# Graph attention kernel: three mask quarters and half of the first graph's heads move from ahead of the steps to between the steps

## The chip, the cores and the metric

The kernel runs on one core of one Trainium2 chip. The metric is the time of one launch in device microseconds (us), the median of several runs. A separate, profiled execution gives the trace; its times are given from the start of its span.

## The reference

Eight graphs of 2048 nodes and 256 channels share one adjacency matrix of 2048 x 2048 integers. For each graph, one attention layer with eight heads of 32 channels, a feed-forward part and three layer norms are computed, all in float32:

```
qkv = einsum('fnc,ck->fnk', x, w_qkv)            # q, k, v: 8 heads of 32
scores = einsum('fnhd,fmhd->fhnm', q, k) / sqrt(32)
scores = where(adj > 0, scores, -1e9)
attn = softmax(scores)
t = einsum('fhnm,fmhd->fnhd', attn, v)
x1 = layernorm(x + t)
x2 = layernorm(x1 + relu(x1 @ w1 + b1) @ w2 + b2)
out = layernorm(x + x2)
```

## The kernel before

**Steps.** The work is cut into 1024 items (f, qc, g, mb): 8 graphs f, 4 quarters qc of 512 query nodes, 2 halves g of the heads (4 heads each) and 16 blocks mb of 128 key nodes. The loop at the end of `fast_path` (L552 on) makes one step per item, in this order. A step t issues the exponentials of item t+1 (L237, ScalarE, 128 x 2048 in one instruction), the scores of item t+2 (`LEAD` is 2), the products with the values of item t (L249, TensorE) and the adding-up of item t (`add_up`). `scores` (L222) is four heads' matmuls on TensorE (L230) and two adds on VectorE (L233), which add the mask and write the sum into a tile `p` of the pool `pp`; the exponentials are made in place in that tile.

**Tiles p.** The pool `pp` has 12 buffers of 128 x 2048 float32. A new tile takes the buffer that has been free longest in program order, and its first writer waits for the last user of the tile before it. The softmax denominators are sums of all exponentials of one (f, qc, g), 16 tiles. `add_up` reduces these 16 to four: blocks 3, 6, 8, 11, 13 and 15 are added into the tile of block 0 on GpSimd (L271), blocks 4, 7, 10 into the tile of block 1 and blocks 5, 9, 12 into that of block 2 by accumulating DMAs that GpSimd issues (L268). Within a chain one accumulation waits for the one ahead of it. So a moved tile's buffer is free when its DMA has landed, and a pooled tile's when GpSimd has added it. `denominator` (L295, matmuls with ones at L310) closes a group a few steps after its last block and frees the other four tiles.

**Masks.** The mask of one quarter qc is the transposed adjacency as fp8 values that are added to the scores: eight pieces of 128 x 2 x 512, each of which serves two blocks mb. `begin` makes all four quarters, in 16 blocks (qc, c) of 512 x 512: a 1 MB load of the adjacency (L511), two conversions to bf16 on VectorE (L528, 128 x 1024 each), 16 transposes on TensorE (L141), and two evictions from PSUM to fp8, one by ScalarE (L147) and one by VectorE (L145). Each piece is written to a DRAM tensor `md` (L148) by the SP queue. The pieces of quarter 0 stay in the pool `mkp` (9 buffers); for every later quarter, and for every later graph, `load_mask` (L150) reads them back, from step 17 of the 32 steps of a quarter on.

**Ahead of the steps.** For the first graph `begin` also loads x (L517), transposes it (`turn_rows`, L95), and makes the queries, keys and values: with block (0, c) those of heads g = 0 (`project`, L200, from `channels` and the value matmuls, all TensorE records at L54), with block (1, c) those of heads g = 1. The scores of items 0 and 1 stand behind block (1, 3); the blocks of quarters 2 and 3 stand behind them and ahead of step 0.

**Side work.** Everything else (projections, transposes, feed-forward, norms of finished quarters, denominators) is written as generators in a list `fill`, sorted by due time. `advance(t)` (L457) resumes them at the head of a step, ahead of that step's scores and values. A generator that needs a PSUM bank yields `BANK`; there is one bank for such work, and a budget (`STEP` 2200 per step, `UNIT` 1024) lets through about one piece per step, which is a group of four 512-column matmuls or as much. When something is needed and not there, `advance(..., finish=True)` runs the list without that limit. `NEXT` (L499) starts the next graph's work at fixed steps. [...]

Of the kernel before, what the change touches and what calls it, by code (L numbers as in the profile page):

```python
# [10 lines left out]
F32 = mybir.dt.float32  # L11
# [8 lines left out]
P = 128  # L20
H = 8
D = 32
CH = 512
# [6 lines left out]
BANK, MORE, WAIT, TURNED, ROOM, INPUTS = -1, -2, -3, -4, -5, -10  # L30
STEP, UNIT, TURN, KEPT = 2200, 1024, 1400, 2200

MASKED = -57344.0
CODE = -5.0


# [25 lines left out]
def fast_path(ctx, tc, cst, x, adj, out, RS):  # L62
# [52 lines left out]
    def take(shape, dt):  # L115
        live.pop(0)
        live.append(ld.tile(shape, dt, name="in"))
        return live[-1]

    def give(t):  # L120
        live[:] = [None if u is t else u for u in live]


    MD = dp.tile([NCK, MB // 2, P, 2 * CH // 4], I32, name="md")
    MK = {}

    def words(mask):
        return mask.rearrange("p b q -> p (b q)").bitcast(I32)

    def mask_piece(t, qc, k):  # L130
        MK[t, qc, k] = mkp.tile([P, 2, CH], F8, name="mask")
        return MK[t, qc, k]

    def mask_blocks(qc, mc, cv, to=None):
        for half in range(2):
            yield BANK
            ps = bank(BF16)
            for r in range(2):
                for j in range(TPC):
                    rr = 2 * half + r  # L140
                    nc.tensor.transpose(ps[:, r, j * P:(j + 1) * P], cv[:, j, rr * P:(rr + 1) * P], identb)  # L141
            k = 2 * mc + half
            m = to[half] if to else mask_piece(0, qc, k)
            if half:
                nc.vector.tensor_tensor(m, ps, cst["ones"][:, 0:1, None].to_broadcast([P, 2, CH]), ALU.min, saturate=False)  # L145
            else:
                nc.scalar.copy(m.bitcast(I8), ps)  # L147
            nc.sync.dma_start(MD[qc, k], words(m))  # L148

    def load_mask(f, qc, k):  # L150
        nc.sync.dma_start(words(mask_piece(f, qc, k)), MD[qc, k])
# [5 lines left out]
    def queries(f, c, xT):  # L157
        for g in range(2):
            yield from channels(QT, qp, "qT", (f, c, g), xT, g * P)

    def turn_rows(xc, xT):
        for a in range(2):
            yield BANK
            ps = bank()
            transposes(ps, [xc[:, j, a * P:(a + 1) * P] for j in range(TPC)])
            nc.scalar.copy(xT[:, a, :], ps)  # L166
# [14 lines left out]
    def channels(store, pool, name, key, xT, k0):  # L181
        yield BANK
        ps = bank()
        for a in range(2):
            if a:
                yield MORE
            columns(ps, wqkv[:, a, k0:k0 + P], xT[:, a, :], start=(a == 0), stop=(a == 1))
        store[key] = pool.tile([P, CH], F32, name=name)
        nc.scalar.copy(store[key], ps)
# [10 lines left out]
    def project(f, c, g, xT=None):  # L200
        if xT is None:
            xT = yield from reload(f, c)
            while len(KT) < (2 * f + g) * NCK + c:
                yield 1
        yield from channels(KT, kp, "kT", (f, c, g), xT, C + g * P)
        yield BANK
        ps = bank()
        for j in range(TPC):
            if j:
                yield MORE  # L210
            for a in range(2):
                columns(ps[:, j * P:(j + 1) * P], xT[:, a, j * P:(j + 1) * P],
                        wqkv[:, a, 2 * C + g * P:2 * C + (g + 1) * P], start=(a == 0), stop=(a == 1))
        v = vp.tile([P, TPC, P], F32, name="v")
        nc.scalar.copy(v, ps.rearrange("p (j c) -> p j c", c=P))
        V[f, c, g] = v
        give(xT)
# [4 lines left out]
    def scores(item):  # L222
        f, qc, g, mb = item
        pt = PT[item] = pp.tile([P, 4, CH], F32, name="p")
        ps2 = [score_pair() for _ in range(2)]

        for half in (1, 0):
            for j in range(2):
                r = D * (2 * half + j)
                nc.tensor.matmul(ps2[half][:, j, :], KT[f, mb // TPC, g][r:r + D, (mb % TPC) * P:(mb % TPC + 1) * P],  # L230
                                 QT[f, qc, g][r:r + D, :], start=True, stop=True)
        for half, ps in enumerate(ps2):
            nc.vector.tensor_tensor(pt[:, 2 * half:2 * half + 2, :], ps,  # L233
                                    MK[f, qc, mb // 2][:, mb % 2, None, :].to_broadcast([P, 2, CH]), ALU.add)

    def exponentials(item):
        nc.scalar.activation(PT[item], PT[item], AF.Exp, scale=1.0 / math.sqrt(D))  # L237
# [249 lines left out]
                resume(e, t)  # L487

    items = [(f, qc, g, mb) for f in range(F) for qc in range(NCK) for g in range(2) for mb in range(MB)]
    LEAD = 2  # L490
    FRAME = 2 * NCK * MB


# [7 lines left out]
            104: [(project, 0, 1)], 108: [(project, 1, 1)], 112: [(project, 2, 1)], 116: [(project, 3, 1)]}  # L501

    def begin():
        todo = deque((qc, c) for qc in range(NCK) for c in range(NCK))
        rows, cols = [], deque()

        def fetch():
            if todo:
                qc, c = todo.popleft()
                t = pp.tile([P, 4, CH], F32, name="p").bitcast(I32)  # L510
                nc.sync.dma_start(t, adj[qc * CH:(qc + 1) * CH, c * CH:(c + 1) * CH].rearrange("(j p) m -> p j m", p=P))  # L511
                cols.append((qc, c, t))

        for c in range(NCK):
            rows.append(pp.tile([P, 4, CH], F32, name="p"))
            xc = rows[c][:, 0:2, :].rearrange("p a (b c) -> p (a b) c", c=C)
            nc.sync.dma_start(xc, x[0, c * CH:(c + 1) * CH, :].rearrange("(j p) c -> p j c", p=P))  # L517
            fetch()
        fetch()
        while cols:  # L520
            qc, c, col = cols.popleft()
            if c % 2 == 0:
                two = pp.tile([P, 4, CH], F32, name="p").rearrange("p a q -> p (a q)").bitcast(BF16)
            cv = two[:, c % 2 * TPC * CH:(c % 2 + 1) * TPC * CH].rearrange("p (j m) -> p j m", m=CH)

            for half, what in enumerate((CODE, MASKED)):
                part = slice(half * 2 * P, (half + 1) * 2 * P)
                nc.vector.tensor_scalar(cv[:, :, part], col[:, :, part], 0.0, what, op0=ALU.is_le, op1=ALU.mult)  # L528
            fetch()
            xT = rows[c][:, 2:4, :]  # L530
            if qc == 0:
                yield from turn_rows(rows[c][:, 0:2, :].rearrange("p a (b c) -> p (a b) c", c=C), xT)
                nc.sync.dma_start(XD[0][c], xT)
                XT[0, c] = xT
                if c == 0:
                    yield from queries(0, 0, xT)
                yield from project(0, c, 0, xT)
            elif qc == 1:
                yield from project(0, c, 1, xT)
            if qc and c % 2 == 0:  # L540
                out4 = take([P, 4, 2, CH], F8)
                give(out4)
            yield from mask_blocks(qc, c, cv, [out4[:, c % 2 * 2 + i] for i in range(2)] if qc else None)
            if (qc, c) == (1, NCK - 1):
                for k in range(LEAD):
                    scores(items[k])
                exponentials(items[0])

    for _ in begin():
        pass  # L550
    state["side"] = 0
    for t, (f, qc, g, mb) in enumerate(items):  # L552
        if g == 1 and mb % 2 and (f + 1 < F or qc + 1 < NCK):
            load_mask(f + (qc + 1) // NCK, (qc + 1) % NCK, mb // 2)
        for what, *which in NEXT.get(t % FRAME, []):
            to = f if what is ask and which[0] else f + 1
            if to < F:
                at = (0, 0, 0) if what is turn else (which[0], 0, 0) if what is ask else (0, which[1], which[0] * TPC)
                start(t, what(to, *which), t + 3 * MB if what is turn else items.index((to, *at)) - LEAD - 1)
        if t == len(items) - MB // 2:  # L560
            state["rows"] = take([P, TPC, C], F32)
            nc.sync.dma_start(state["rows"], x[f, qc * CH:(qc + 1) * CH, :].rearrange("(p j) c -> p j c", p=P))
        if t:
            advance(t)

        if t + 1 < len(items):
            exponentials(items[t + 1])
        if t + LEAD < len(items):
            nf, _, ng, nmb = items[t + LEAD]
            t0 = t  # L570
            while (nf, nmb // TPC, ng) not in V:
                advance(t0, finish=True)
                t0 += 1
            scores(items[t + LEAD])
        values(items[t])
        add_up(items[t])
        if mb == LAST:
            start(t + 2, denominator(f, qc, g, t + SUM), t + SUM + 4)
# [241 lines left out]
```

## Time and profile before

| | |
|---|---|
| median of 3 runs | 3248.77 us (3247.61 to 3251.02) |
| the profiled execution's own time | 3242.05 us |
| its span | 3240.0 us |
| TensorE / VectorE / ScalarE / GpSimd busy | 3101.0 / 2739.5 / 2435.5 / 2593.3 us |
| exponentials of item 0 and item 1 start | 62.38 us, 94.78 us |
| exponentials of item 32, 64, 96, 128, 160 start | 180.4, 276.3, 370.2, 466.1, 560.8 us |
| exponentials of the last item start | 3171.9 us |

The starts of the exponentials are read from the timeline of ScalarE: the records at L237 are counted in order of time, one per item. They are the milestones by which this document compares stages. In the groups of the profile, a row gives line, engine, operation, output and inputs, the count, the busy time and the mean of one in ns, and then the idle time of that engine just ahead of these instructions and what ended it. A float32 matmul has two records, so eight records at L230 or L249 are one step's four heads.

### The profile page before, as it was taken

To read this page: it belongs to the slowest core of one execution; us is meant where nothing else is said; L and a number is where in the kernel's file an instruction comes from. 1 tells how busy PE (TensorE), PEld (TensorE's weight loads), DVE (VectorE), ACT (ScalarE), POOL (GpSimd) and SP (SyncE) were. 2 spreads that over 40 slices of the span, in tenths; PEclk is the share of its full clock that TensorE was granted. 3 is DMA by queue.
4 is the path that set the end of the run, shared out by engine and by line. 5 is a ranking of instruction groups with operands and counts; after the bars stand their busy time and mean duration, and the time that the engine had idled before them with its cause. 6 is when DMAs were issued, how large, how long until landed. Compare 5 with 4: busy or idle time off the path is not lost.

```text
span 3240.0 us, 68306 instructions
## 1 busy us (share of the span) xinstructions
PE 3101.0 (96%) x28948; PEld 976.0 (30%) x28948; DVE 2739.5 (85%) x3203; ACT 2435.5 (75%) x1937; POOL 2593.3 (80%) x1357
## 2 busy tenths in 40 slices
PE   7899999999999999999999999999999999998994
PEld 4222333323332233322333323323233323332221
DVE  4888888888888888888988888888888888888994
ACT  3667778778778777778777778777778777777773
POOL 0568888788878888788887888888888788878894
PEclk8899999999999999999999999999999999999997
DMA  9688779778879788788788879878788878877773
GB/s 322 147 179 190 182 175 202 176 174 200 181 176 205 171 190 193 158 195 200 177 181 175 184 181 220 177 167 197 175 192 194 180 171 201 181 171 160 168 160 78
DMA packets 153384, 591.57 MB, mean 183 GB/s; under 512 B 15056, under 2 KB 67792, under 8 KB 103920
## 3 DMA queue, kind: packets, MB, share of 16 engines
q0 software_dynamic: 64560, 435.85, 67.2%
q1 hardware_dynamic: 87696, 149.98, 13.1%
q8 instruction: 229, 3.75, 0.4%
q10 hardware_dynamic: 816, 1.31, 0.1%
q14 instruction: 83, 0.68, 0.1%
HBM read 146.67 MB, written 37.75 MB: 57 GB/s over the span
## 4 chain that ended last, share of the span: by engine, by line
PE 75%; DVE 8%; POOL 5%; DMA 4%; issue 4%; ACT 2%; DVEq 0%; ACTq 0%; POOLq 0%
PE s L230 28%; PE x L249 24%; PE x L54 13%; DVE p L233 6%; PE x L310 6%; PE x L95 4%; DMA p<-p 3%; POOL p L271 2%; ACT p L237 2%; DMA mask<-md 1%; POOL y L357 1%; DVE st L278 1%; POOL y L355 0%; POOL y L414 0%; POOL y L412 0%
## 5 line engine op out<-in xcount | busy, mean ns | idle before, releaser
L233 DVE TENSOR_TENSOR p<-s,mask 128x1024 f32<-128x1024 f32 x2048 | 2410.5, 1219 | 360.3 <-PE s L230 202.9
L237 ACT ACTIVATE p<-p 128x2048 f32<-128x2048 f32 x1024 | 1956.3, 1910 | 510.2 <-DVE p L233 456.7
L271 POOL TENSOR_TENSOR p<-p 128x2048 f32<-128x2048 f32 x382 | 1829.5, 4791 | 216.0 <-ACT p L237 213.8
L230 PE MATMUL s<-qT,kT 32*128 32x512 f32 x8192 | 1171.2, 641 | 34.1 <-DVE p L233 29.1
L249 PE MATMUL x<-p,v 128*32 128x512 f32 x8192 | 1092.9, 606 | 16.7 <-ACT p L237 16.7
L268 POOL DMA_DIRECT2D p<-p x384 | 360.1, 957 | 305.5 <-ACT p L237 95.5
L230 PEld LDWEIGHTS s<-qT,kT 32*128 32x128 f32 x8192 | 320.5, 183 | 637.8 <-DVE p L233 580.1
L249 PEld LDWEIGHTS x<-p,v 128*32 128x32 f32 x8192 | 161.3, 108 | 796.4 <-issue 302.6
L310 PE MATMUL x<-p,ones 128*32 128x512 f32 x2016 | 261.1, 594 | 15.9 <-POOL p L271 9.7
L289 ACT ACTIVATE y<-y,nb,rs 128x256 f32<-128x256 f32 x372 | 219.2, 590 | 46.1 <-POOL nb L286 46.1
L54 PE MATMUL x<-in,wqkv 128*32 128x512 f32 x1888 | 243.5, 592 | 0.0
L278 DVE BATCH_NORM_STATS2 st<-y 128x6 f32<-128x256 f32 x372 | 155.2, 417 | 6.2 <-DMA y<-in_x_dram 6.2
L54 PE MATMUL x<-w2s,hT 128*32 128x256 f32 x2048 | 122.8, 381 | 3.3 <-DVE y L436 2.3
L54 PE MATMUL x<-turned,w1s 128*32 128x512 f32 x992 | 122.9, 592 | 0.4 <-ACT in L166 0.4
L54 PEld LDWEIGHTS x<-wqkv,in 128*32 128x32 f32 x3584 | 102.2, 110 | 63.5 <-issue 59.0
L54 PE MATMUL x<-wqkv,in 128*32 128x128 f32 x3584 | 117.2, 273 | 0.0
L310 PEld LDWEIGHTS x<-p,ones 128*32 128x32 f32 x2016 | 64.1, 110 | 171.4 <-issue 136.0
L54 PEld LDWEIGHTS x<-in,wqkv 128*32 128x32 f32 x1888 | 61.7, 110 | 140.9 <-issue 113.7
L283 POOL TENSOR_TENSOR rs<-rs,mhalf 128x4 f32<-128x4 f32 x93 | 97.1, 1044 | 7.7
L54 PEld LDWEIGHTS x<-w2s,hT 128*32 128x32 f32 x2048 | 66.1, 110 | 76.5 <-issue 30.3
L414 POOL TENSOR_TENSOR y<-y,be1b2r 128x1024 f32<-128x1024 f32 x32 | 85.4, 2667 | 0.6
L355 POOL TENSOR_TENSOR y<-y,g2r 128x1024 f32<-128x1024 f32 x31 | 82.7, 2668 | 1.2 <-ACT y L289 1.2
(117 smaller groups left out, 1333.1 us busy)
## 6 DMA issues: line engine op xcount, KB each, us to landing
p<-p POOLq DMA_DIRECT2D x384, 1024.0 KB, 10.5
in<-xd SPq DMA_DIRECT2D x87, 512.0 KB, 10.7
mask<-md SPq DMA_DIRECT2D x248, 128.0 KB, 8.0
y<-in_x_dram POOLq DMA_DIRECT2D x62, 512.0 KB, 8.0
p<-in_adj_dram SPq DMA_DIRECT2D x16, 1024.0 KB, 9.7
out_dram<-y SPq DMA_DIRECT2D x31, 512.0 KB, 6.4
in<-in_x_dram SPq DMA_DIRECT2D x29, 512.0 KB, 15.9
xd<-in SPq DMA_DIRECT2D x28, 512.0 KB, 10.9
```

The costliest lines, as they stand in the source:

```text
L54: nc.tensor.matmul(out[r:r + D], lhsT[:, r:r + D], rhs, start=start, stop=stop)
L95: nc.tensor.transpose(ps[:, j * P:(j + 1) * P], s, ident)
L230: nc.tensor.matmul(ps2[half][:, j, :], KT[f, mb // TPC, g][r:r + D, (mb % TPC) * P:(mb % TPC + 1) * P], QT[f, qc, g][r:r + D, :], start=Tr ...
L233: nc.vector.tensor_tensor(pt[:, 2 * half:2 * half + 2, :], ps, MK[f, qc, mb // 2][:, mb % 2, None, :].to_broadcast([P, 2, CH]), ALU.add)
L237: nc.scalar.activation(PT[item], PT[item], AF.Exp, scale=1.0 / math.sqrt(D))
L249: nc.tensor.matmul(O[grp][r:r + D, :], V[f, mb // TPC, g][:, mb % TPC, r:r + D], PT[item][:, h, :], start=(mb == 0), stop=(mb == LAST))
L268: nc.gpsimd.dma_start(PT[f, qc, g, chain[0]], PT.pop(item), accum_op=ALU.add)
L271: nc.gpsimd.tensor_tensor(first, first, PT.pop(item), ALU.add)
L278: nc.vector.bn_stats(st, t[:, j, :])
L283: nc.gpsimd.tensor_tensor(rs, rs, cst["mhalf"], ALU.pow)
L289: nc.scalar.activation(t[:, j, :], t[:, j, :], AF.Identity, bias=nb[:, j:j + 1], scale=rs[:, j:j + 1])
L310: nc.tensor.matmul(ps[r:r + D, :], cst["ones"], term[:, h, :], start=(n == 0), stop=(n == len(terms) - 1))
```

## The change

`begin` now makes only quarter 0 of the masks and only heads g = 0 of the first graph, and issues the first scores right after. Both evictions of a transposed block are ScalarE's. The four projections of heads g = 1 (with the queries of g = 1 for quarter 0) become a generator `other_half`, one for each c, due at steps 13, 17, 21 and 25. The 12 remaining blocks become generators `mask_quarter(qc + 1, c)`, started at blocks mb 0, 4, 8 and 12 of the g = 0 groups of the first three quarters of graph 0. Each takes one tile `p`, loads its 1 MB into it as two 512 KB DMAs, converts in place five steps later, and transposes, evicts and writes out from the same tile, in two pieces of side work. So a tile `p` is held from the load to the second write to `md`. The four tiles that hold the transposed rows of x are held until their `other_half` has run. `load_mask` is issued six steps later than before (`LATE`), in all graphs, and in graph 0 only after its piece was made. The mask value of VectorE's eviction, `MASKED`, goes.

```diff
+    def mask_quarter(qc, c):
+        t = pp.tile([P, 4, CH], F32, name="p").rearrange("p a q -> p (a q)")
+        half = TPC * CH // 2
+        parts = [t[:, h * half:(h + 1) * half] for h in range(2)]
+        cvs = []
+        for h, part in enumerate(parts):
+            col = part.bitcast(I32).rearrange("p (j m) -> p j m", j=TPC)
+            nc.sync.dma_start(col, adj[qc * CH:(qc + 1) * CH, (2 * c + h) * 2 * P:(2 * c + h + 1) * 2 * P].rearrange("(j p) m -> p j m", p=P))
+        yield 5
+        for part in parts:
...
+            convert(cv, part.bitcast(I32).rearrange("p (a b m) -> p a b m", a=2, b=2))
+            yield 1
+        for h, part in enumerate(parts):
             yield BANK
             ps = bank(BF16)
...
+            turn_mask(ps, cvs[h])
+            m = part[:, half // 4:half // 2].bitcast(F8).rearrange("p (b q) -> p b q", b=2)
+            nc.scalar.copy(m.bitcast(I8), ps)
+            nc.sync.dma_start(MD[qc, 2 * c + h], words(m))
+            MADE.add((qc, 2 * c + h))
...
-    LEAD = 2
+    LEAD, LATE = 2, 6
...
     def begin():
...
+        for c in range(NCK):
...
+            yield from turn_rows(rows[c][:, 0:2, :].rearrange("p a (b c) -> p (a b) c", c=C), xT)
+            nc.sync.dma_start(XD[0][c], xT)
+            XT[0, c] = xT
+            if c == 0:
+                yield from channels(QT, qp, "qT", (0, 0, 0), xT, 0)
+            yield from project(0, c, 0, xT)
+            for half in range(2):
+                ps = bank(BF16)
+                turn_mask(ps, [cv[:, j, half * 2 * P:(half + 1) * 2 * P] for j in range(TPC)])
+                m = mask_piece(0, 0, 2 * c + half)
+                nc.scalar.copy(m.bitcast(I8), ps)
+                nc.sync.dma_start(MD[0, 2 * c + half], words(m))
+                MADE.add((0, 2 * c + half))
+        for k in range(LEAD):
+            scores(items[k])
+        exponentials(items[0])
+        for c in range(NCK):
+            start(0, other_half(c, rows[c][:, 2:4, :]), MB + TPC * c - LEAD - 1)
...
     for t, (f, qc, g, mb) in enumerate(items):
-        if g == 1 and mb % 2 and (f + 1 < F or qc + 1 < NCK):
-            load_mask(f + (qc + 1) // NCK, (qc + 1) % NCK, mb // 2)
+        uf, uqc, ug, umb = items[max(t - LATE, 0)]
+        if ug == 1 and umb % 2 and (uf + 1 < F or uqc + 1 < NCK):
+            while ((uqc + 1) % NCK, umb // 2) not in MADE:
+                advance(t, finish=True)
+            load_mask(uf + (uqc + 1) // NCK, (uqc + 1) % NCK, umb // 2)
+        if f == 0 and mb % TPC == 0 and qc + 1 < NCK:
+            c = g * TPC + mb // TPC
+            if c < NCK:
+                start(t, mask_quarter(qc + 1, c), t + MB + 2)
```

More of the change, by code (lines that the diff above doesn't have):

```diff
@@ L31 @@
 STEP, UNIT, TURN, KEPT = 2200, 1024, 1400, 2200
-MASKED = -57344.0
 CODE = -5.0
@@ L124, in fast_path @@
     MD = dp.tile([NCK, MB // 2, P, 2 * CH // 4], I32, name="md")
-    MK = {}
+    MK, MADE = {}, set()
     def words(mask):
@@ L132, in mask_piece, with turn_mask, convert @@
         return MK[t, qc, k]
-    def mask_blocks(qc, mc, cv, to=None):
-        for half in range(2):
+    def turn_mask(ps, cv):
+        state["credit"] -= 2 * TURN
+        for r in range(2):
+            for j in range(TPC):
+                nc.tensor.transpose(ps[:, r, j * P:(j + 1) * P], cv[j][:, r * P:(r + 1) * P], identb)
+    def convert(cv, col):
+        nc.vector.tensor_scalar(cv, col, 0.0, CODE, op0=ALU.is_le, op1=ALU.mult)
+    def mask_quarter(qc, c):
[8 more added lines that the diff above has]
+        for part in parts:
+            cv = part.bitcast(BF16).rearrange("p (a b m) -> p a b m", a=2, b=4)[:, :, 0:2, :]
+            cvs.append([cv[:, j // 2, j % 2] for j in range(TPC)])
+            convert(cv, part.bitcast(I32).rearrange("p (a b m) -> p a b m", a=2, b=2))
+            yield 1
+        for h, part in enumerate(parts):
             yield BANK
             ps = bank(BF16)
[L138 to L148, printed above, removed]
+            turn_mask(ps, cvs[h])
[3 more added lines that the diff above has]
+            MADE.add((qc, 2 * c + h))
     def load_mask(f, qc, k):
@@ L503, in begin @@
     def begin():
[L504 to L512, printed above, removed]
+        rows, cols = [], []
         for c in range(NCK):
@@ L517, in begin @@
             nc.sync.dma_start(xc, x[0, c * CH:(c + 1) * CH, :].rearrange("(j p) c -> p j c", p=P))
[L518 to L521, printed above, removed]
+            cols.append(pp.tile([P, 4, CH], F32, name="p").bitcast(I32))
+            nc.sync.dma_start(cols[c], adj[0:CH, c * CH:(c + 1) * CH].rearrange("(j p) m -> p j m", p=P))
+        for c in range(NCK):
             if c % 2 == 0:
@@ L524, in begin, with other_half @@
             cv = two[:, c % 2 * TPC * CH:(c % 2 + 1) * TPC * CH].rearrange("p (j m) -> p j m", m=CH)
-            for half, what in enumerate((CODE, MASKED)):
+            for half in range(2):
                 part = slice(half * 2 * P, (half + 1) * 2 * P)
-                nc.vector.tensor_scalar(cv[:, :, part], col[:, :, part], 0.0, what, op0=ALU.is_le, op1=ALU.mult)
-            fetch()
+                convert(cv[:, :, part], cols[c][:, :, part])
             xT = rows[c][:, 2:4, :]
[L531 to L547, printed above, removed]
+            yield from turn_rows(rows[c][:, 0:2, :].rearrange("p a (b c) -> p (a b) c", c=C), xT)
[4 more added lines that the diff above has]
+            yield from project(0, c, 0, xT)
+            for half in range(2):
+                ps = bank(BF16)
[9 more added lines that the diff above has]
+            start(0, other_half(c, rows[c][:, 2:4, :]), MB + TPC * c - LEAD - 1)
+    def other_half(c, xT):
+        if c == 0:
+            yield from channels(QT, qp, "qT", (0, 0, 1), xT, P)
+        yield from project(0, c, 1, xT)
     for _ in begin():
```

## The prediction, as put on record

> **What bounds the kernel now.** I read the page first: its busy times say TensorE.
>
> ```profile
> PE 3101.0 (96%) x28948; PEld 976.0 (30%) x28948; DVE 2739.5 (85%) x3203; ACT 2435.5 (75%) x1937; POOL 2593.3 (80%) x1357
> PEclk8899999999999999999999999999999999999997
> ```
>
> An average over stages, so next the stretches before and after the steps begin (columns: TensorE busy, weight loads, VectorE, ScalarE, GpSimd, granted clock, DMA share, GB/s).
>
> ```profile
> 60.00:80.00 20.00, 9.25 (x72) 6.80 (x72) 13.75 (x16) 5.96 (x5) 0.00 (x0) 0.54 0.79 272
> 80.00:100.00 20.00, 11.54 (x84) 7.52 (x88) 12.15 (x15) 5.86 (x5) 0.00 (x0) 0.52 0.30 93
> 160.00:180.00 20.00, 17.65 (x136) 4.45 (x130) 18.50 (x16) 16.14 (x10) 14.71 (x8) 1.00 1.04 229
> 180.00:200.00 20.00, 15.40 (x112) 3.59 (x112) 12.12 (x11) 10.39 (x7) 13.70 (x4) 0.91 0.83 199
> ```
>
> From 60 to 95 us nothing is near its limit: the last two mask quarters pass through VectorE, TensorE and an eviction one block after another, one in 3.8 us (conversions at 88.20 and 92.06). That is the time the change aims at. Around 180 us there is another hole. The timeline shows its kind:
>
> ```profile
> 190.76 4.52 POOL L271 TENSOR_TENSOR p<-p 128x2048 f32<-128x2048 f32 x1 [2.30 <-ACT p L237]
> ...
> 193.98 0.16 PEld L310 LDWEIGHTS x<-p,ones 128*32 128x32 f32 x8 [5.09 <-DMA p<-p]
> 193.98 1.20 PE L310 MATMUL x<-p,ones 128*32 128x512 f32 x8 [4.18 <-DMA p<-p]
> 195.11 0.52 PEld L230 LDWEIGHTS s<-qT,kT 32*128 32x128 f32 x8 [0.97 <-issue]
> 195.11 2.09 PE L230 MATMUL s<-qT,kT 32*128 32x512 f32 x8
> ```
>
> A late accumulating DMA holds in-order TensorE, and its next instructions take twice their time (2.09 us, not 1.07). In the steps the chain of waits gives 1.07 us for a step's scores, 1.00 for its values and 0.86 for a full side piece: 2.93 us. Without a side piece a step takes 2.55 us, set by VectorE's adds (starts at 127.81, 130.35, 132.91).
>
> How late a tile's buffer comes free is the third thing to read: the first additions of the run on GpSimd, and the row of all tiles p between 96 and 466 us.
>
> ```profile
> 105.17 4.56 POOL L271 TENSOR_TENSOR p<-p 128x2048 f32<-128x2048 f32 x1 [85.46 <-ACT p L237]
> 109.67 1.84 POOL L268 DMA_DIRECT2D p<-p  x2
> DMA to landing us min/median/max: 6.8/10.8/15.6
> ```
>
> Alone an accumulation lands in 7 us; the pair issued from 109.67 had both landed at 123.1, 13.4 us later; the median is 10.8.
>
> **What the Trainium skill says.** "DMA: Bandwidth & Descriptors", SWDGE vs HWDGE: accumulating during a DMA is GpSimd's alone, so L268 can't leave the queue that also adds (L271); and the section "Issuing engines are not separate DMA queues": all queues share the 16 DMA engines. The trace agrees: at a DMA share of 1.04 (160 to 180 us) accumulations took 11 to 16 us. "TensorE: Matmul & The Clock Gate", Part 1: an idle window of about 3.4 us halves the clock; here 0.54 and 0.52 above, and 2.09 us after a hole of 5. "Perfetto Trace Analysis", Optimization Strategy: bubbles that repeat can mean that there is no buffer for the next tile. Before, adds hardly wait for buffers (0.9 us for DMAs between 96 and 466 us).
>
> **The change, part by part** (minus is gain; by the profiled execution, 3242.05 us, span plus 2.05).
>
> *Earlier start.* Before, block (0, 3) left TensorE at 38.96 us. Both evictions are now ScalarE's, 1.01 us each in one queue ahead of the next rows' copies, which have no slack: 3 x 1.07 = 3.2 us later, 42.2. Scores 1.1 and adds 2.5: item 0's exponentials at 45.8, item 1's at 48.4, not 94.78: **-46.4**. The loads of these blocks stand as before on SP, so they don't move.
>
> *TensorE work brought between the steps.* Four projections of 3.46 us (keys 2 x 0.86, values 2 x 0.87), a query piece 1.72, 24 half blocks of 0.54 (16 transposes took 1.07 at 32.08): 13.8 + 1.7 + 12.9 = **+28.4**. By the order of instructions all of it stands ahead of item 160; from there both programs issue the same. The steps there are TensorE's, so it adds fully, except for 18 of the first 32 steps: these had no side piece before and went at VectorE's pace, and all have one now: 18 x (2.55 - 2.07) = **-8.6**. The hole at 194 us should go, as slower steps leave the DMAs time: **-6**. A step with one of the 24 conversions (0.65 us) needs 2.48 + 0.65 = 3.1 of VectorE against 2.93: 24 x 0.2, half of it hidden: **+2**. The 24 casts (1.01) I cost at nothing, since ScalarE idles 25%; without that cover they'd cost 24. Sum without buffers: **-31**.
>
> *Buffers p.* Counting tiles from allocation to last use in program order, before at most 6 of 12 are held in the first 16 steps (heads of the chains, tiles in work), so a buffer is reused 9 items after its tile was given back. After, row tiles and blocks bring this to 10 or 11 through step 21: item 6 takes item 3's buffer, 7 takes 4's, 8 takes 5's, 10 takes 7's, 12 takes 9's, 16 takes 12's. The wait stands on VectorE's add; behind it are the next adds and conversions, on TensorE the next scores (for PSUM), and the exponentials that feed the next accumulation. A moved tile needs exponentials 1.9, queue and landing 7 to 13, but has two steps, 5.9 us. Item by item, from the start of item 0's exponentials: those of item 3 end at 9.7; GpSimd adds to 14.4 (4.7); accumulation 4 lands at 21.4 (+7.0), 5 at 27.8 (14.4 + 13.4). Item 7's adds start at 21.4 (17.0 unhindered), item 8's at 27.8, item 9 runs to 33.1. Accumulation 7 lands 5.5 after 27.8 and 2.7 later for a 1 MB block load: item 10 at 36. Addition 8 ends at 36.9, accumulation 9, with 10 behind it, lands at 45.5: item 12 there, not at 40.5. Accumulation 12 lands near 58.7: item 16. Items 15 and 20 take buffers of blocks, free when the write to `md` lands (3 to 8 us): +3 for item 20; items 24 and 26 +1 each. TensorE restarts slowly after four of these holes, about +0.8 each. So item 32's exponentials start at 45.8 + 117 = 163; unhindered 48.4 + 31 x 2.93 + 2.6 (three steps with a double piece) = 142: **+21**. In quarters 1 and 2 blocks again take tiles and 4 MB of loads (10.8 us of all DMA engines on top of about 40 in 47): reuse distance 3 to 6, accumulations about 3 us later; by the same working waits of 2.3, 1.2, 2 and 4 us in items 43 to 47, and the like in items 70 to 80: **+9 each**. Sum **+39**.
>
> *Mask reads.* Six steps later, 17.6 us; they are then 7 steps, 20.5 us, ahead of use and land in 8.1 (24.8 at most): **0**; without that cover some us a quarter.
>
> Total -31 + 39 = **+8**: 3250 for a profiled run. The median of the runs is 6.7 above the profiled execution, so 3248.8 + 8 = **3257**.
>
> The disputed size is the waits: at landings of 7 us and quick writes the first group costs 14 and the others 4 each (22); at 15.6 us each, 40 and 15 each (70). I take 39: solo landings in the stalled group, the shared pair where two overlap.
>
> **Rivals.** (1) *Faster: the early start outlives the waits.* If buffer waits stay under 31 us in all, time falls; at 15 us, as when TensorE catches up at VectorE's 2.5 us a step after each hole, 3233. For it: an idle front of 35 us is real, and before no buffer wait is seen. Against: the reuse distance falls from 9 to 3. (2) *Slower by much: DMAs bind.* With 53 us of transfers in a 47 us group, chained accumulations slip as at 178 us (15.6), waits reach 63: 3281. Against: the block loads come early, when no accumulation runs. (3) *Even*: waits near 31, 3249. (4) *Not done*: steps don't start sooner because SP's block loads hold `begin`. Against: TensorE waited for such a load only once before, at 19 us.
>
> **How the numbers follow.** Forecast 0.50 (3250 to 3268), rival 1 0.24, rival 2 0.14, rival 3 0.10, rival 4 0.02. About 0.2%, 6.5 us, is what can be told from no change. Faster by over that: most of rival 1, 0.21. Within: rival 3 and the edges of the forecast and rival 1, 0.25. Slower: 0.54. The forecast's own range and the rivals' centres give 3231 to 3284.
>
> **What would show it.** Item 1's exponentials at 48; item 32 near 163 (142 if rival 1); VectorE idle at the adds ended by DMA or GpSimd at tiles p, some 20 us before item 32 (0.9 before); item 160 near 569, not 561, and from there equal lengths. Item 160 under 550 makes the prediction wrong.

## The result, and the profile after

The changed kernel takes 3266.5 us (median of 6 runs, 3262.86 to 3274.01), the kernel before 3248.31 in the same job (6 runs, 3247.05 to 3251.02). The ratio is 1.0061, 95% interval 1.0051 to 1.0070: 18 us slower, more than twice the 8 that were forecast. That is on the forecast's side and near the upper end of its range (3250 to 3268).

In the page of the changed kernel, the lines that answer to the two shown of before:

```profile
PE 3108.9 (95%) x28948; PEld 976.5 (30%) x28948; DVE 2741.3 (84%) x3187; ACT 2448.8 (75%) x1953; POOL 2594.8 (79%) x1357
PEclk9999999999999999999999999999999999999997
```

The totals hardly differ. The clock row no longer begins with two eights: the slow front is gone. What came for it is below the row's resolution (one slice is 82 us), so here are stretches of 20 us of the changed kernel, the first two of them at the times shown of before:

```profile
60.00:80.00 20.00, 14.53 (x148) 4.61 (x144) 10.62 (x10) 8.83 (x7) 8.96 (x6) 0.83 0.77 156
80.00:100.00 20.00, 15.52 (x172) 5.91 (x168) 12.83 (x13) 11.78 (x8) 11.47 (x6) 0.91 0.90 200
...
200.00:220.00 20.00, 14.52 (x104) 3.98 (x102) 13.29 (x10) 11.69 (x9) 11.20 (x5) 0.83 1.03 247
320.00:340.00 20.00, 11.35 (x86) 3.78 (x86) 18.23 (x14) 10.21 (x10) 14.08 (x5) 0.74 0.75 184
```

(The columns are those of the stretches of before: busy TensorE, weight loads, VectorE, ScalarE, GpSimd, granted clock, DMA share, GB/s.) At 60 to 100 us the steps now run, though with holes. At 200 to 220 us TensorE is idle a quarter of the time while the DMA engines are full (1.03). At 320 to 340 us TensorE is idle for 8.7 us and VectorE is busy for 18.2 of the 20: another kind of hole. That suggests two causes, and the milestones (starts of the exponentials, by item) say how much each stage lost, in us. The forecast's column is taken from its working: 142 - 48.4 - 85.6 = +8 and +21 for waits in the first stage, -6 and +9 in the second, +9 in the third. What is left of the TensorE work (28.4 - 8.6 + 2 - 8) is put at the stage up to item 160; the working says only that it stands ahead of that item.

| stage | before | after | difference | forecast |
|---|---|---|---|---|
| start to item 1 | 94.8 | 48.6 | -46.2 | -46.4 |
| item 1 to 32 | 85.6 | 113.9 | +28.3 | +29 |
| 32 to 64 | 95.9 | 107.0 | +11.1 | +3 |
| 64 to 96 | 93.9 | 113.4 | +19.5 | +9 |
| 96 to 160 | 190.6 | 206.8 | +16.2 | +13.8 |
| 160 to the last | 2611.1 | 2606.8 | -4.3 | 0 |
| sum | 3171.9 | 3196.5 | +24.6 | +8.4 |

The sum of two single traces is 24.6, the medians differ by 18.2. The profiled run of before was 6.7 us under its median and that of after (3266.33) at its own, so about 6 us of this table can't be given to a stage. Some of it lies in the first row: in the traces of E2, E3, E4 and E11 below, which share before's front, item 1 starts at 96.4 to 97.9 us, not at 94.8.

First kind of hole: VectorE's waits (total in us, times, longest), of before between 96 and 466 us and then of the change between 45 and 383 us.

```profile
DVE p L233 <- DMA p<-p: 0.9, 1, 0.9
...
DVE p L248 <- DMA p<-p: 22.1, 9, 6.4
DVE p L248 <- PE s L245: 21.5, 31, 1.9
DVE p L248 <- DMA md<-p: 5.1, 3, 2.5
...
DVE p L248 <- POOL p L286: 1.3, 2, 0.8
```

L248 (L233 in before) is the mask add that first writes a new tile `p`. It waits for an accumulation, a write to `md` or a pooled add to give the buffer back: 28.5 us, where before had 0.9. 19.5 of it lies ahead of item 32. Its first four, from VectorE's timeline:

```profile
69.36 2.36 DVE L248 TENSOR_TENSOR p<-s,mask 128x1024 f32<-128x1024 f32 x2 [6.38 <-DMA p<-p]
74.23 2.36 DVE L248 TENSOR_TENSOR p<-s,mask 128x1024 f32<-128x1024 f32 x2 [1.92 <-DMA p<-p]
82.41 2.35 DVE L248 TENSOR_TENSOR p<-s,mask 128x1024 f32<-128x1024 f32 x2 [2.62 <-DMA p<-p]
90.99 4.84 DVE L248 TENSOR_TENSOR p<-s,mask 128x1024 f32<-128x1024 f32 x4 [2.77 <-DMA p<-p]
```

These are items 7, 8, 10 and 12. The prediction had them at 21.4, 27.8, 36 and 45.5 us after 45.8, which is 67.2, 73.6, 81.8 and 91.3. The later and smaller waits of this stage stand at items 15, 20, 24 and 26 (1.3, 1.3, 1.6 and 0.9 us), all of which the prediction names; at item 16, which it names too, none is seen.

Second kind: the conversions. Their row in before (up to 200 us: busy time, mean ns), their summary in the change (L140: shortest, median and longest in ns, first and last start), and the worst of them in the timeline of VectorE, GpSimd and TensorE:

```profile
L528 DVE TENSOR_SCALAR p<-p 128x1024 bf16<-128x1024 int32 x32 | 20.8, 692 | 12.8 <-DMA p<-in_adj_dram 12.8
...
L140 DVE TENSOR_SCALAR p<-p x32: 675/684/9233, 19.3 to 345.2; 128x1024 bf16<-128x1024 int32 x32
```

```profile
318.70 3.22 POOL L370 TENSOR_TENSOR y<-y,g2r 128x1024 f32<-128x1024 f32 x1
319.99 9.23 DVE L140 TENSOR_SCALAR p<-p 128x1024 bf16<-128x1024 int32 x1
321.03 5.34 POOL L286 TENSOR_TENSOR p<-p 128x2048 f32<-128x2048 f32 x1
325.50 3.16 POOL L372 TENSOR_TENSOR y<-y,be2r 128x1024 f32<-128x1024 f32 x1
...
330.41 2.09 PE L245 MATMUL s<-qT,kT 32*128 32x512 f32 x8 [8.65 <-DVE p L248]
```

The median conversion takes 0.684 us. This one starts while GpSimd is in an instruction and ends 0.56 us after the third of three in a row (325.50 + 3.16 = 328.66; 319.99 + 9.23 = 329.22). Behind it in VectorE's order stand the mask adds, so TensorE waits 8.65 us, and its next scores take 2.09 us instead of about 1.1. Of the 24 conversions between the steps, five are stretched like this (4.38, 3.53, 4.07, 3.31, 9.23 us) and one slightly (1.10). These six, and none of the other 18, started while GpSimd was in an add or multiplication of two tiles. Above 0.68 us each, the 24 take 3.7 us too much ahead of item 32, 6.7 in quarter 1 and 11.2 in quarter 2, 21.6 in all. In before no conversion stood beside GpSimd's adds of tiles `p`: all were done before the steps. The Trainium skill ("SBUF — State Buffer", section "Who interferes with whom") describes it: VectorE and GpSimd share a pair of ports that is taken for a whole instruction, `tensor_scalar` is among those that can use it, and "the other **fully blocks** (not throttle)". The trace agrees, with 4.38 us where GpSimd's one add ended 3.83 us after the conversion's start and 9.23 us where three followed each other. The prediction took the duration from rows without such a neighbour.

### The profile page after: what moved, and what is told of

Same layout as the page of the kernel before. It is cut to its first block, busy times and chain, and to the rows that moved or that the text cites. A ratio compares the mean times of both kernels' runs of the same rounds, so it can differ in the third digit from the quotient of the medians.

```text
span 3264.5 us, 68367 instructions
## 1 busy us (share of the span) xinstructions
PE 3108.9 (95%) x28948; PEld 976.5 (30%) x28948; DVE 2741.3 (84%) x3187; ACT 2448.8 (75%) x1953; POOL 2594.8 (79%) x1357
## 4 chain that ended last, share of the span: by engine, by line
PE 72%; DVE 4%; POOL 3%; issue 3%; ACT 1%; DMA 1%; DVEq 0%; ACTq 0%; POOLq 0%
PE s L245 26%; PE x L264 23%; PE x L53 14%; PE x L325 5%; PE x L94 4%; DVE p L248 3%; POOL p L286 1%; ACT p L252 1%; POOL y L372 1%; DMA p<-p 0%; POOL y L370 0%; DVE st L293 0%; DVE y L360 0%; POOL y L374 0%; DMA y<-in_x_dram 0%
## 5 line engine op out<-in xcount | busy, mean ns | idle before, releaser
L248 DVE TENSOR_TENSOR p<-s,mask 128x1024 f32<-128x1024 f32 x2048 | 2409.3, 1218 | 410.6 <-PE s L245 215.6
L325 PE MATMUL x<-p,ones 128*32 128x512 f32 x2016 | 260.5, 595 | 12.7 <-POOL p L286 10.5
L53 PE MATMUL x<-w2s,hT 128*32 128x256 f32 x1920 | 115.4, 381 | 0.0
L372 POOL TENSOR_TENSOR y<-y,be2r 128x1024 f32<-128x1024 f32 x31 | 84.2, 2715 | 0.0
```

Source lines behind the costliest of these rows:

```text
L53: nc.tensor.matmul(out[r:r + D], lhsT[:, r:r + D], rhs, start=start, stop=stop)
L325: nc.tensor.matmul(ps[r:r + D, :], cst["ones"], term[:, h, :], start=(n == 0), stop=(n == len(terms) - 1))
L372: nc.gpsimd.tensor_tensor(z, z, rows(cst["be2r"]), ALU.add)
```

## Experiments

Ratios are to before in the same job, with 95% intervals; differences in us are of the medians. The expectation of E5 says how it changes the computation; E7 and E8 take over the same form.

**E1, the conversions without the shared port.**

```diff
-            convert(cv, part.bitcast(I32).rearrange("p (a b m) -> p a b m", a=2, b=2))
+            nc.vector.tensor_scalar(cv, part.bitcast(I32).rearrange("p (a b m) -> p a b m", a=2, b=2), 0.0, None,
+                op0=ALU.is_le, op1=ALU.add, accum_out=small.tile([P, 1], F32, name="acc"))
...
-            nc.scalar.copy(m.bitcast(I8), ps)
+            nc.scalar.mul(m.bitcast(I8), ps, CODE)
```

> The changed kernel, but each conversion of a mask block between the steps also sums its output (so it compares only; ScalarE's eviction multiplies by the code). Theory A (the conversion, in the form it has, can't run beside a large GpSimd instruction, and VectorE stands until that ends; together with the waits for tiles p this is the loss): the 24 conversions take 1.1 to 1.3 us each and none is stretched, where the changed kernel has five of 3.3 to 9.2 us; item 160's exponentials start 10 to 20 us sooner than its 589.7; time 3248 to 3257, against 3266.5. Theory B (the waits for tiles p alone are the loss; a stretched conversion only stands where the next add would have waited for a buffer anyway): item 160 within 4 us of 589.7, time 3263 to 3270.

Measured: 3267.02 us, ratio 1.0056 (1.0044 to 1.0069), as slow as the change, with item 160 at 591.9 us: the figures of theory B. The group of its conversions (busy time, mean ns), and VectorE's waits between 45 and 385 us:

```profile
L154 DVE TENSOR_SCALAR_CACHE_REDUCE p<-p 128x1024 bf16<-128x1024 int32 x24 | 29.0, 1208 | 0.0
```

```profile
DVE p L248 <- DMA p<-p: 27.5, 10, 6.3
...
DVE p L248 <- DMA md<-p: 9.4, 4, 3.7
```

None is stretched (1.185 to 1.221 us), though seven of them started during an instruction of GpSimd. That is what the same section says of the form that writes its accumulator. VectorE spends 29 us on them and not 38, but waits 37 us for DMAs and not 27. The stretch is real and not the whole cause: without it no time came back.

**E2, the conversions alone**, on the kernel before, with an unused result. By the order of VectorE's instructions each stands one step ahead of where the change has it (steps 5, 6, 8, 9 and so on, not 6, 7, 9, 10).

```diff
+        if t in (5, 6, 8, 9, 12, 13, 16, 17, 36, 37, 40, 41, 44, 45, 48, 49, 68, 69, 72, 73, 76, 77, 80, 81):
+            nc.vector.tensor_scalar(spare, wqkv[:, :, 0:CH].bitcast(I32), 0.0, CODE, op0=ALU.is_le, op1=ALU.mult)
```

> The kernel before, with 24 conversions of 128 x 1024 added on VectorE (from the weights into a spare tile), at the 24 steps of graph 0 at which the changed kernel has its own; no tile p is taken. Theory A: some are stretched to 3 us and more while GpSimd adds, 10 us or more above 24 x 0.68 in sum, and the time rises by 5 to 15 us, to 3254 to 3263. Theory B: each takes 0.7 us, half hidden: 3248 to 3253.

Measured: 3295.13 us, ratio 1.0134 (1.0119 to 1.0149): +47, three times the most that was expected. One of them in its timeline, with the add that it met:

```profile
116.81 4.54 POOL L272 TENSOR_TENSOR p<-p 128x2048 f32<-128x2048 f32 x1 [1.18 <-ACT p L238]
117.50 4.40 DVE L567 TENSOR_SCALAR spare<-wqkv 128x1024 int8<-128x1024 int32 x1
```

It starts 0.69 us into the add and ends 0.55 after it. The 24 take 46 us together, 30 of it stretch; eleven were hit here, six in the change. Stage by stage the time of the conversions is nearly the time lost: 17, 14 and 15 us of conversions, and 18, 12 and 15 us more from item 1 to 32, to 64 and to 96. So not only the stretch stood in the steps' path, but the plain 0.68 us of each as well.

**E3, the buffers alone**, on the kernel before: 16 extra tiles `p`, held over the steps for which the change holds its rows and blocks (given back one step sooner, by the order of TensorE's instructions), each touched by a tiny DMA and a tiny write.

```diff
+        for a, b in HOLD:
+            if t == a:
+                held[b] = pp.tile([P, 4, CH], F32, name="p")
+                nc.sync.dma_start(held[b][:, 0, 0:4], x[0, 0:P, 0:4])
+            if t == b:
+                nc.vector.memset(held.pop(b)[:, 0, 0:1], 0.0)
```

> The kernel before, with 16 further tiles p allocated and given back at the steps of graph 0 at which the changed kernel allocates and gives back its blocks and its four row tiles; each is only touched by a DMA of 16 bytes per partition and, at its end, by one short VectorE write. Theory A: waits of VectorE for DMAs at tiles p rise from 0.9 us to 15 to 25 us; the kernel is slower by 15 to 25 us: 3263 to 3273. Theory B, in which buffers are all of the loss: slower by 35 to 45 us, 3283 to 3293. If buffers cost nothing: 3248.

Measured: 3275.84 us, ratio 1.0079 (1.0066 to 1.0092): +27, between the two theories' ranges and nearer to A's. VectorE's waits between 96 and 402 us:

```profile
DVE p L233 <- DMA p<-p: 29.2, 10, 4.6
```

Held buffers alone make the waits that the prediction described, without any block load: 12.9 us of them (with one for GpSimd) ahead of item 32, 9.4 and 8.5 in the next two quarters. The stages lost 17.0, 3.3 and 9.7 us from item 1 to 32, to 64 and to 96. The working's terms for buffers and for the hole at 194 us, which is gone in E3 too, give 21, 9 - 6 = 3 and 9.

**E11, both on the kernel before** (the edits of E2 and E3 together).

> The kernel before, early start and all else as it was, with both single costs that were measured apart: the 24 extra conversions on VectorE (their result unused, alone +46 us) and the 16 extra buffers held (alone +26 us). If they stand in different steps they add: 3315 to 3325 us. If a wait for a buffer and a conversion cover each other: 3293 to 3305 us.

Measured: 3290.87 us, ratio 1.0137 (1.0122 to 1.0152): +43, far below the 74 of a sum (47 and 27, where the expectation has 46 and 26) and no more than the conversions alone. VectorE's waits between 97 and 417 us:

```profile
DVE p L234 <- DMA p<-p: 13.5, 5, 4.5
```

The waits fell from 29.2 to 13.5 us and the stretch from 30 to 22. My reading is that accumulations catch up while VectorE stands in a stretched conversion, and that GpSimd's add ends while it waits for a buffer; no run separates this. Shown is that the two don't add, and that both shrank when they stood together.

**E5, the conversions on ScalarE.**

```diff
-            convert(cv, part.bitcast(I32).rearrange("p (a b m) -> p a b m", a=2, b=2))
+            nc.scalar.activation(cv, part.bitcast(I32).rearrange("p (a b m) -> p a b m", a=2, b=2), AF.Identity,
+                bias=cst["code"][:, 0:1], scale=-CODE)
```

> The changed kernel with the 24 conversions between the steps on ScalarE (-5 + 5 x adjacency, which takes the adjacency as 0 or 1). They took 38 us of VectorE in the changed kernel, 16 of work and 22 of standing beside GpSimd. Theory A (conversions stand in the steps' path for nearly their whole time, as they did when added alone): 20 to 35 us less, 3232 to 3247, item 160 at 560 or sooner. Theory B (the waits for tiles p cover them: without conversions VectorE waits for the buffers instead): 0 to 10 us less, 3256 to 3267, VectorE's waits for DMAs at tiles p longer by about as much.

Measured: 3270.5 us, ratio 1.0074 (1.0061 to 1.0087). VectorE has nothing of the conversions left, and waits between 45 and 385 us:

```profile
DVE p L248 <- DMA p<-p: 37.6, 10, 6.4
...
DVE p L248 <- DMA md<-p: 14.6, 4, 5.0
```

That is 52 us of waits for buffers in place of 27: what E11 showed from the other side, and more than theory B had it, for no time came back. Not all of it need be VectorE's absence: ScalarE is busy 254 us between items 1 and 96 where it was busy 230, and the exponentials, which feed the accumulations, start later behind their adds (28 us in sum, 20 in the change). How much of the new waits comes from that is open.

**E6, the heads ahead again** (the masks between the steps alone) and **E10, only the heads between the steps** (all masks ahead, as before).

```diff
             yield from project(0, c, 0, xT)
+            yield from other_half(c, xT)
...
-        for c in range(NCK):
-            start(0, other_half(c, rows[c][:, 2:4, :]), MB + TPC * c - LEAD - 1)
...
```

This is the edit of E6; E10 makes the heads by the same `other_half`, on the kernel before.

> The changed kernel with the second half of the heads made ahead of the steps again (and a missing query tile forced like a missing value tile). The steps start 15.5 us later; the four row tiles are free by then, so 8 tiles p at most are held in the first 16 steps, not 11. Theory A (of the 21 us of waits before item 32 most come from the row tiles): waits in the first group fall to about 7 us, side work of 15.5 us leaves the steps, item 32 within 3 us of the changed kernel's 162.5, and 8 to 15 us less in all for what is then not owed later: 3252 to 3258. Theory B (blocks and their conversions alone make the loss): as the changed kernel, 3263 to 3270.

> The kernel before with the other part of the change alone: all masks are made ahead as before, and only the second half of the first graph's heads is made between steps. If the two parts simply add, this is worth what taking it out of the changed kernel cost (3278.3 against 3266.5, so 12 us): 3235 to 3239 us. If the heads cost between the steps what they cost ahead of them (item 1 about 10 us earlier, item 32 as before), 3245 to 3251 us: the 12 us of the other run then came from the masks between meeting the heads, not from the heads.

E6: 3278.32 us, ratio 1.0100 (1.0085 to 1.0114), slower than the change. E10: 3253.72, ratio 1.0020 (1.0013 to 1.0028). Both expectations missed in both runs. The heads between the steps cost 6 us alone and save 12 in company, so the parts don't add either.

E10 prices the heads' terms one by one. Item 1 comes at 93.6 us, 1.2 earlier than in before's trace and 2.8 to 4.3 earlier than in the four others with its front: as long as the masks of quarters 2 and 3 stand ahead, the heads there cost little. Items 1 to 32 take 8.1 us more (forecast: 13.8 + 1.7 - 8.6 = 6.9). Items 32 to 64 take 5.4 less, which looks like the hole (forecast -6), but only in part is: TensorE's wait for the late DMA fell from 4.2 to 0.7 us, and it ran 698 instructions there where before ran 753. In all it ran 151 fewer between items 32 and 128, and 156 more in items 128 to 160 (1104 for 948), which took 10.0 us more. The side work that the heads displaced comes back there, and the working has no term for it. From item 1 to 160 the heads cost 9.2 us, where 6.9 - 6 = 0.9 was forecast.

E6 gains 9.4 us on the change up to item 32 counted from item 1, but starts 10.6 later, and loses 10.2 and 12.1 in quarters 1 and 2. Its longest single wait, at item 46 in VectorE's timeline, and the landing of its four writes to `md` that were issued between 195 and 230 us:

```profile
223.92 2.35 DVE L248 TENSOR_TENSOR p<-s,mask 128x1024 f32<-128x1024 f32 x2 [17.68 <-DMA md<-p]
```

```profile
DMA to landing us min/median/max: 9.2/15.1/21.1
```

A block's buffer is given back only when its last write has landed. The write that this add waited for was issued at 202.7, right behind two 512 KB block loads that landed 15.5 and 21.2 us after issue, and a reload. In the change the longest such wait is 2.5 us. Why heads between the steps spare it, beyond other moments of loads and writes, is not settled.

**E9, the writes to `md` from ScalarE's queue**, to take them out of the order in which SyncE issues its DMAs.

```diff
-            nc.sync.dma_start(MD[qc, 2 * c + h], words(m))
+            nc.scalar.dma_start(MD[qc, 2 * c + h], words(m))
```

> The changed kernel, with the finished mask pieces' write to DRAM (md from p) issued by ScalarE, right behind the cast that makes them, and not by SyncE, where in the trace of after it stands behind block loads that wait for a buffer. Theory A (SyncE's order keeps the blocks' buffers, and VectorE waits for them): VectorE's waits for DMA md from p (10.6 us in all in after) go to under 3 us, those for DMA p from p shrink, quarters 1 and 2 (items 32 to 96, 220 us in after) get 6 to 12 us shorter: 3254 to 3261 us. Theory B (the DMA engines themselves are full there, and who issues doesn't matter): waits only change names, 3263 to 3270 us.

Measured: 3270.46 us, ratio 1.0068 (1.0055 to 1.0080). (VectorE waits 5.1 us for `md` in the change, not the 10.6 of the expectation.) That wait is 7.5 us here, the one for accumulations 21.1, items 32 to 96 take 220.9 us and took 220.4. SyncE's order isn't the cause: without it the waits are as long, and the writes land in 8.5 us (median between 160 and 385 us), in the change in 8.3. That leaves the full DMA engines, which is argued here and not shown.

**E7 and E8, blocks half as often.** Blocks start every eight steps over both halves of the heads, with conversions on ScalarE; E8 has the heads ahead as in E6.

```diff
-        if f == 0 and mb % TPC == 0 and qc + 1 < NCK:
...
+        if f == 0 and mb % (2 * TPC) == 0 and qc + 1 < NCK:
+            start(t, mask_quarter(qc + 1, g * 2 + mb // (2 * TPC)), t + MB // 2 + 2)
```

> As the run with conversions on ScalarE, and the blocks of a quarter started every 8 steps over both halves of the heads, not every 4 in the first half, due 10 steps later. Held tiles p in the groups of quarters 1 and 2 fall from 8 to 6 or 7 (7 to 10 in the first groups). If tiles are what is left: 5 to 12 us less than the run with ScalarE alone. If not: within 4 us of it.

> All three: conversions on ScalarE, blocks every 8 steps, the second half of the heads ahead of the steps. If conversions and tiles are the whole loss, what is left is the earlier start less the work brought between the steps: 20 to 30 us faster than the kernel before, 3219 to 3229. If something else is lost too (DMAs of the blocks beside the accumulations), 3235 to 3250.

E7: 3274.32 us, ratio 1.0089 (1.0072 to 1.0107), within 4 us of E5 as the second of its expectations had it. VectorE waits 21.9 us for accumulations and 16.7 for `md` (one of 13.3). E8: 3256.6, ratio 1.0028 (1.0019 to 1.0037), the best of this family, still behind before and slower than either expectation. Waits for accumulations are down to 9.6 us there and those for `md` to 1.0. In their place TensorE waits for a reload of the next graph's rows that landed 28.8 us after issue, right behind a block load:

```profile
210.80 1.93 PE L53 MATMUL x<-in,wqkv 128*32 128x512 f32 x8 [15.20 <-DMA in<-xd]
```

**E4 and E12, the late mask reads**: `LATE` = 6 alone on the kernel before, and taken out of the change.

```diff
-    LEAD, LATE = 2, 6
+    LEAD, LATE = 2, 0
```

> The kernel before, with the reads of the mask pieces issued six steps later, in all graphs. Both theories: no change, 3245 to 3252, since the smallest distance between landing and first use in the kernel before is 20 us and six steps are 17.6 us. If late reads cost anything, 1 us in each of 31 quarters gives 3280.

> The changed kernel with one of its three parts undone: a mask piece's read into SBUF is issued at its own step again, as before the change, and not six steps later. If the late reads are worth in the changed kernel what they were worth alone on the kernel before (7 us gained), it gets that much slower: 3271 to 3277 us. If my prediction's zero holds here, or the gain belongs to the first graph's steps that the stalls have taken over: 3263 to 3269 us. If the early reads collide with block loads and accumulations in quarters 1 and 2, items 32 to 96 take over 224 us where they took 220.

E4: 3241.91 us (10 runs, 3237.12 to 3247.49), ratio 0.9977 (0.9968 to 0.9987): faster than both kernels, and the best version found, where no change was expected. Its profiled run took 3245.96 us, at the slow end of its runs, and the table's stages from item 1 on are within about 1 us of before's. So it doesn't show where the 7 us come from; that stays open. E12: 3286.85, ratio 1.0127 (1.0105 to 1.0149), 20 us slower than the change and slower than any of its expectations. Here the trace tells where. Lines of its timeline, at items 26 and 46:

```profile
143.80 2.35 DVE L248 TENSOR_TENSOR p<-s,mask 128x1024 f32<-128x1024 f32 x2 [2.13 <-PE s L245]
...
151.14 1.14 PE L245 MATMUL s<-qT,kT 32*128 32x512 f32 x8
...
152.35 1.23 DVE L248 TENSOR_TENSOR p<-s,mask 128x1024 f32<-128x1024 f32 x1 [6.19 <-PE s L245]
...
227.09 2.36 DVE L248 TENSOR_TENSOR p<-s,mask 128x1024 f32<-128x1024 f32 x2 [11.49 <-DMA md<-p]
```

By the code, an early read that finds its piece not made runs the whole side list at once (the loop on `MADE`). The trace agrees: pieces of keys and of values and two half blocks stand between two steps on TensorE (143.6 to 151.1 us). Counted against the change, E12 falls behind from 1.7 to 8.9 us at item 26, to 11.2 at item 30, and from 10.2 to 18.2 at item 46, of which 4 come back.

## Why the prediction was right, and where its sizes were not

The forecast had the direction and the main mechanism, tiles `p` that are held longer and buffers that come free late. Its sum of +8 came out of sizes that were wrong both ways.

*The start, right.* Item 1 at 48.6 us; forecast 48.4.

*Buffers ahead of item 32, right in kind, place and size.* Item 32 at 162.5 us; forecast 163. Each of the first four waits came within 2.2 us of its place. The waits there are 19.5 us against 21, with 3.7 of stretch beside them that the working did not have. E3 confirms held tiles as a cause by themselves.

*"A step with one of the 24 conversions (0.65 us) needs 2.48 + 0.65 = 3.1 of VectorE against 2.93: 24 x 0.2, half of it hidden: +2": this is the step that failed.* The duration came from rows where GpSimd was idle, and half was taken as hidden. Beside GpSimd's instructions the same instruction took up to 9.23 us: 21.6 us of stretch in the trace of the change, 30 in E2, where hardly anything was hidden: 46 us of conversions, 47 lost.

*"+9 each" in quarters 1 and 2, not as forecast.* The waits for buffers there were 7.9 and 1.2 us, and with the stretch (6.7 and 11.2) 14.6 and 12.4: in quarter 2 the stretch stands where the waits were forecast. Of the 18.6 us by which the two quarters missed (8.1 and 10.5), this gives 9.0 (27.0 against 18). The other 9.6 are not told apart. The same stages of before (three lines) and of the change (three lines), items 32 to 64, 64 to 96 and 128 to 160, columns as above:

```profile
180.40:276.30 95.90, 90.12 (x753) 25.57 (x752) 79.00 (x80) 70.51 (x51) 68.63 (x30) 0.98 0.80 175
276.30:370.20 93.90, 93.68 (x884) 29.35 (x880) 84.06 (x98) 75.06 (x60) 82.91 (x45) 1.00 0.86 187
466.10:560.80 94.70, 94.70 (x948) 30.52 (x944) 84.09 (x98) 74.38 (x59) 83.37 (x44) 1.00 0.85 181
...
162.50:269.50 107.00, 95.02 (x736) 28.53 (x732) 89.86 (x88) 77.49 (x58) 64.11 (x29) 0.94 0.77 188
269.50:383.00 113.50, 98.53 (x804) 30.02 (x800) 99.97 (x106) 80.23 (x66) 84.37 (x44) 0.92 0.83 195
477.60:589.70 112.10, 108.78 (x1260) 39.28 (x1260) 84.53 (x98) 78.79 (x67) 82.71 (x43) 1.00 0.79 174
```

In both quarters TensorE was busy some 4.9 us longer with fewer instructions, at a lower granted clock (0.94 and 0.92, before 0.98 and 1.00). That is about the size of what is left, but no run tests it.

*TensorE's work, right in place, its credits too large.* It stands ahead of item 160 as forecast: items 96 to 160 took 16.2 us more for 13.8, all of it in items 128 to 160 (1260 instructions for 948). But the working took off 8.6 us for steps without a side piece and 6 for the hole, and in E10 these came to 6.3 in all (15.5 us of work cost 9.2), as displaced side work came back later. The casts on ScalarE hardly show: between 45 and 385 us TensorE's denominators wait 0.9 us for them and VectorE's adds 1.3.

*Mask reads at 0: the cover held.* No wait for a mask is among VectorE's. Yet their move is no neutral edit: alone it gains 7 us, and without it the change would be 20 slower.

*Lengths from item 160 on, equal within 4.3 us*: 288.8 for 289.5 us to item 256, and 3.6 us shorter beyond. Item 160 came at 589.7, not 569, which is mostly the two quarters' miss.

*Rivals, and some luck.* The first rival's condition was met: the waits were 28.5 us, under the 31 at which the prediction's own sum is even. The time rose all the same, by the stretch and by the credits, which the prediction had at other sizes, so its sign in the change's own trace is in part luck. In E5, without conversions on VectorE, the waits were 52 us and the time 23 above before, so buffers may make it slower alone; ScalarE's share in that is open. The second rival had the DMAs full, as they are at 200 to 220 us, but waits of 63 us did not come. (The prediction's reading of 11 to 16 us for accumulations at 160 to 180 us in before is a little high: the four issued then took 9.1 to 15.6.) That one cause hides the other was in no rival.

## What to carry to other kernels

Price an instruction by a row in which the neighbours that it will have are busy; a conversion of 0.68 us took up to 9.2 beside another engine's work. When work moves between steps, count for how long it holds buffers, up to the landing of its last write. Two causes that stall the same engine may cover each other: test each alone and both together (47, 27 and 43 us here), before trusting that the removal of one brings its time back. And when one stage gets shorter, see whether it did less work that a later stage then does (698 instructions for 753, and later 1104 for 948).

## What the runs showed of the hardware

- A `tensor_scalar` from int32 to bf16 or int8 (128 x 1024, 0.68 us) that started during a GpSimd instruction on two SBUF tiles ended some 0.55 us after it: six times in the change, eleven in E2. Twice it came after GpSimd's next instructions only, which followed at once (9.23 and 5.50 us); once, in E11, it came ahead of the next one. The same operation with an accumulator took 1.21 us, and none of 24 was stretched, seven of them during an instruction of GpSimd.
- A 128 KB write from SBUF to DRAM took 21 us to land in E6, behind 1 MB of block loads and a 512 KB reload, at a DMA share of 1.03 (195 to 225 us); in the change the quickest took 1.7. Issued from ScalarE's queue the writes took 8.5 us in the median, from SyncE's 8.3.
